# Splitting roped queries into high and low float32r parts ahead of the per-head key projection in a one-core decoder layer

## The chip, the cores and the metric

The kernel runs on one core of one Trainium2 chip. The metric is device time in microseconds (us) for one execution of the whole layer; several executions are timed and their median is compared. One more execution is taken under the hardware profiler, and all durations below come from that one.

## The reference, cut to what matters

The layer takes 1024 tokens (16 sequences of 64) of width 256 and adds three sublayers to them: self-attention over quantised weights, cross-attention with a compressed context, and a mixture of 16 experts. The change lies in the cross-attention:

```python
q_hk = (hidden_q @ Wq.T).reshape(Bv, Sv, H, K)             # 16 heads of 128
q_big = jnp.einsum('bshk,hkq->bshq', q_hk, w_kc_q)         # 192 per head
q_big = _apply_rope(q_big, sin_q, cos_q)                   # a half rotated against the other
q_r = jnp.einsum('bshq,hqr->bhsr', q_big, W_qr)            # 64 per head
k_r = jnp.einsum('bld,hdr->bhlr', kv_r, W_kr)
scores = jnp.einsum('bhsr,bhlr->bhsl', q_r, k_r)
attn = jax.nn.softmax(scores, axis=-1)
ctx_c = jnp.einsum('bhsl,bld->bhsd', attn, kv_r)
```

The kernel multiplies W_qr by W_kr ahead of time, so that the roped query of a head, 192 long, is multiplied by one 192 x 64 matrix and then meets the context itself.

## The kernel before, in words

The program runs in three stages: self-attention (to about 205 us of the span), cross-attention (to about 415 us), then routing and experts. Instructions are emitted by Python helpers in a program order; a planner that simulates the engines then fixes one order for each engine. `issue_after` and `after` pin some instructions behind others. An engine works through its own order and waits at whatever instruction is not ready. The planner may move work of the next unit ahead of work that would wait.

**Units.** Cross-attention works on a quad of four heads and a half of the tokens (512) at a time. `units` (L1117) lists eight such units. The loop at L1121 runs as a pipeline: in iteration n it computes the rotated queries of unit n (`rotated_queries`), the per-head product and scores of unit n-1 (`pair_queries`, `pair_scores`), and the context and output projection of unit n-2 (`pair_context`, `cross_project`).

**Rotated queries.** The four heads have 4 x 96 = 384 first-half and 384 second-half query entries. They are laid out in three tiles t of 128 rows, each with two halves ab. For each t and ab six float32r matmuls (a float32 product made of high and low parts, three passes for each of two chunks) fill one PSUM tile `mm`, of which there are four. VectorE multiplies it by two rope tables (`rt` tiles, L976); GpSimd subtracts or adds two of them (L982) into a float32 tile `roped`. The generator yields after each t, so the three tiles are spread over an iteration.

**Per-head product.** A head's 96 rows do not fit the 128-row tiles: tile 0 holds head 0 and the start of head 1, tile 1 the rest of head 1 and the start of head 2, tile 2 the rest of head 2 and head 3. `w_s` holds for each tile t, each of two blocks blk (the two heads in it) and each ab a 128 x 64 matrix with zeros in the rows of the other head. `pair_queries` (L988) runs 12 float32 matmuls for a unit, each of 64 output columns; the two of a (t, ab) write the two halves of the PSUM partitions. ScalarE copies the sums to `q_r` (L1008), and L1020 multiplies them by the context.

**Weights of a quad.** `quad_steps` (L403) loads six raw matrices through SyncE's queue into the single-buffered `raw` tiles, zeroes `w_s` on GpSimd (L422), makes `w_q` with L431 and the blocks of `w_s` with L453 (PE) and L463 (VectorE copies out of PSUM). Each raw tile must be released by its readers before the next quad's load.

`three` and `parts_of` (L107 to L113) are the helpers of the float32r scheme: `parts_of` copies to the high part on ScalarE and subtracts on VectorE or the engine that is named.

## Time and profile before

| | us |
|---|---|
| median of 3 runs | 569.73 (569.17 to 570.04) |
| profiled execution, its own time | 570.74 |
| its span | 569.0 |
| PE busy in the span | 537.4 |
| VectorE / ScalarE / GpSimd busy | 400.9 / 279.3 / 230.5 |
| mean granted TensorE clock | 0.984 |

The profile's page gives busy time by engine, the chain of work that ended last, and the costliest groups of instructions. A float32 matmul appears as two records, a float32r matmul as one. Two 64-column matmuls into different halves of the PSUM partitions overlap, so the mean duration of one record is longer than what a record adds. PE is TensorE, PEld its weight loads, DVE VectorE, ACT ScalarE, POOL GpSimd, SP SyncE.

### The profile page before, as it was taken

What the parts mean: (1) busy time and instruction counts of PE and PEld (TensorE: products, weight loads), DVE (VectorE), ACT (ScalarE), POOL (GpSimd) and SP (SyncE); (2) the same over time, 40 slices, a digit from 0 to 9 for tenths busy, and PEclk for the clock granted to TensorE, in tenths of its full rate; (3) what the DMA queues carried; (4) which work ended last, traced back from release to release, by engine and by line L of the source; (5) the groups of instructions that cost most, each with busy time, mean ns of one, the idle gap of its engine ahead of it and who ended that gap; (6) DMA issues with size and microseconds to landing.
All of it is one profiled execution on the core that took longest, in us unless ns stands there. A gap on an engine that the chain in (4) does not pass through costs nothing.

```text
span 569.0 us, 10603 instructions
## 1 busy us (share of the span) xinstructions
PE 537.4 (94%) x4013; PEld 444.5 (78%) x4013; DVE 400.9 (70%) x879; ACT 279.3 (49%) x524; POOL 230.5 (41%) x213
## 2 busy tenths in 40 slices
PE   7999999999999998999999999999999879999961
PEld 6888898988989876667687676676788779999961
DVE  5456555644555788767485686888878678999876
ACT  4677556575565533131323324143445368777551
POOL 4160500102000104434441445453445738888862
PEclk9999999999999999999999999999999989999995
DMA  8654431724300499564010000000322667776374
GB/s 213 163 170 129 129 106 44 205 95 108 97 1 1 119 289 277 140 188 127 2 52 20 8 1 1 0 30 1 105 106 80 209 217 255 244 249 239 123 272 164
DMA packets 44262, 70.83 MB, mean 124 GB/s; under 512 B 11824, under 2 KB 25232, under 8 KB 44208
## 3 DMA queue, kind: packets, MB, share of 16 engines
q1 hardware_dynamic: 39376, 58.71, 34.7%
q0 software_dynamic: 3696, 10.36, 4.7%
q10 hardware_dynamic: 1136, 1.05, 0.6%
q8 instruction: 33, 0.54, 0.4%
q14 instruction: 21, 0.17, 0.1%
HBM read 48.61 MB, written 21.86 MB: 124 GB/s over the span
## 4 chain that ended last, share of the span: by engine, by line
PE 76%; DVE 11%; DMA 4%; issue 3%; ACT 3%; POOL 1%; SPq 0%; DVEq 0%; ACTq 0%; POOLq 0%
PE mm L104 45%; PE mm L997 7%; PE av L582 5%; PE at L565 4%; PE av L104 3%; PE at L343 3%; PE at L1020 2%; PE av L1033 2%; PE mm L431 2%; DMA yd<-y,to 2%; ACT w L278 1%; DMA w<-in_W 1%; DVE hp L113 1%; DVE w L283 1%; DVE x L1326 1%
## 5 line engine op out<-in xcount | busy, mean ns | idle before, releaser
L982 POOL TENSOR_TENSOR roped<-rt,rt 128x512 f32<-128x512 f32 x48 | 62.6, 1326 | 83.3 <-DVE rt L976 80.4
L976 DVE TENSOR_TENSOR rt<-mm,rope_q 128x512 f32<-128x512 f32 x96 | 61.4, 684 | 24.3 <-PE mm L104 23.6
L104 PE MATMUL mm<-xn,w_q 128*128 128x512 f32 x288 | 73.9, 403 | 0.5 <-ACT xn L222 0.5
L104 PEld LDWEIGHTS mm<-xn,w_q 128*128 128x128 f32 x288 | 52.2, 188 | 14.1 <-issue 1.8
L104 PE MATMUL mm<-xs,w 128*128 128x384 f32 x270 | 54.2, 348 | 6.0 <-ACT xs L112 3.0
L1296 POOL DMA_INDIRECT yd<-y,to x45 | 48.7, 1082 | 19.4 <-ACT y L1291 8.0
L104 PEld LDWEIGHTS mm<-xs,w 128*128 128x128 f32 x270 | 47.0, 193 | 8.3 <-ACT xs L112 4.0
L327 ACT ACTIVATE p<-p 128x512 f32<-128x512 f32 x32 | 20.1, 629 | 62.3 <-DVE p L326 62.3
L324 DVE TENSOR_REDUCE sm_m<-at 128x8 f32<-128x512 f32 x32 | 21.8, 680 | 36.1 <-PE at L565 35.2
L997 PE MATMUL mm<-roped,w_s 128*64 128x512 f32 x192 | 46.4, 601 | 0.7 <-POOL roped L982 0.7
L514 POOL TENSOR_TENSOR wv<-code,scale 128x512 fp32r<-128x512 f32 x7 | 9.0, 1282 | 87.4 <-DMA scale<-in_scales 50.3
L605 DVE TENSOR_TENSOR x<-mm,x 128x256 f32<-128x256 f32 x64 | 26.0, 419 | 24.0 <-PE mm L104 22.8
L104 PE MATMUL mm<-wo,o 128*128 128x256 f32 x256 | 39.6, 295 | 0.0
L104 PE MATMUL mm<-xn,wq 128*128 128x512 f32 x128 | 34.6, 404 | 0.7 <-ACT xn L222 0.5
L104 PE MATMUL av<-w,hp 128*128 128x256 f32 x225 | 35.0, 289 | 0.3 <-ACT y L1291 0.3
L104 PE MATMUL mm<-wv,xn 128*128 128x256 f32 x256 | 35.2, 288 | 0.0
L104 PE MATMUL mm<-xn,wk 128*128 128x512 f32 x128 | 34.9, 405 | 0.0
L582 PE MATMUL av<-pt,v 128*128 128x128 f32 x256 | 34.5, 277 | 0.0
L104 PEld LDWEIGHTS mm<-wo,o 128*128 128x128 f32 x256 | 32.9, 190 | 1.5 <-issue 0.4
L582 PEld LDWEIGHTS av<-pt,v 128*128 128x128 f32 x256 | 32.0, 191 | 1.2
L104 PEld LDWEIGHTS mm<-wv,xn 128*128 128x128 f32 x256 | 31.8, 189 | 0.9
L514 POOL TENSOR_TENSOR wo<-code,scale 128x512 fp32r<-128x512 f32 x8 | 10.9, 1368 | 52.0 <-PE mm L104 39.6
(216 smaller groups left out, 1163.8 us busy)
## 6 DMA issues: line engine op xcount, KB each, us to landing
w<-in_W SPq DMA_DIRECT2D x15, 640.0 KB, 4.2
code<-in_codes SPq DMA_DIRECT2D x32, 256.0 KB, 4.4
scale<-in_scales SPq DMA_DIRECT2D x32, 256.0 KB, 4.9
xr<-xd SPq DMA_DIRECT2D x15, 408.0 KB, 4.9
xd<-zeros SPq DMA_DIRECT2D x8, 720.0 KB, 6.8
yd<-zeros SPq DMA_DIRECT2D x8, 512.0 KB, 6.6
got<-yd SPq DMA_DIRECT2D x16, 256.0 KB, 3.6
wq<-in_Wq SPq DMA_DIRECT2D x4, 512.0 KB, 3.7
```

The lines of the kernel that those rows point to most:

```text
L104: m = nc.tensor.matmul(ps, lhsT=l, rhs=r, start=(n == 0), stop=(n == len(pairs) - 1))
L324: nc.vector.tensor_reduce(m, sc, AX.X, ALU.max)
L327: exps.append(nc.scalar.activation(p, p, AF.Exp, scale=scale).ins)
L343: last = nc.tensor.transpose(ps[:, 2 * n : 2 * n + 2, :].rearrange("p a q -> p (a q)"), pn[:, 2 * n : 2 * n + 2, :].rearrange("p a k -> p ...
L514: mults[n] = eng.tensor_tensor(w, *loaded[gr].pop(n), ALU.mult).ins
L565: nc.tensor.matmul(sc[par * 64 : par * 64 + 64, 2 * g + pp, :], lhsT=qk[0][:, b * S : (b + 1) * S], rhs=qk[1][:, b * S : (b + 1) * S], sta ...
L582: nc.tensor.matmul(av[:, k * 128 : (k + 1) * 128], lhsT=v[:, i, k0 : k0 + HD], rhs=pt[:, i].rearrange("p a q -> p (a q)"), start=True, sto ...
L605: nc.vector.tensor_tensor(x[i], ps, x[i], ALU.add)
L976: nc.vector.tensor_tensor(mt, ps3, rope_table(t, 2 * ab + k), ALU.mult)
L982: nc.gpsimd.tensor_tensor(r.rearrange("p (b s) -> p b s", s=S), one, two, op)
L997: nc.tensor.matmul(ps[h // 2][(h % 2) * 64 : (h % 2) * 64 + 64], lhsT=w_s[:, t, blk, ab, :], rhs=roped[2 * t + ab], start=first[h], stop=l ...
L1296: sent = nc.gpsimd.indirect_dma_start(out=yd[: (E - 1) * SLOTS + min(TOPK, E - 1 - e) * NT], out_offset=bass.IndirectOffsetOnAxis(ap=to[:, ...
```

## The change

Tiles 0 and 2 are no longer kept in float32. After the add, GpSimd's result is split by `parts_of` into a float32r high part (`roped`, a ScalarE copy) and a low part (`ropel`, a GpSimd subtraction). For these two tiles the two 64-column blocks of a pair become one 128-column matrix, itself split into high and low parts (`w_sp`), and the product runs as three float32r passes for each ab. Tile 1, whose heads belong to different pairs, keeps its four float32 matmuls. The order of the tiles becomes 0, 2, 1. Each pair's sixth pass is issued after the matmuls of tile 1. `quad_steps` builds the 128-column matrices in the raw tile `wkq` (`whole`), and splits them from there. To make room, `c_t` has three buffers in place of four, and the on-chip scratch for dynamic transfers is set to 8192 bytes.

```diff
-            w_s = pool.tile([128, 3, 2, 2, DC], F32, tag="w_s", name="w_s")
+            w_s = pool.tile([128, 2, 2, DC], F32, tag="w_s", name="w_s")
+            t = pool.tile([128, 2, 2, 4 * DC], F32R, tag="w_sp", name="w_sp")
+            w_sp = [t[:, 0], t[:, 1]]
             nc.gpsimd.memset(w_s, 0.0)
...
+            whole = raw_tile("wkq", [128, 2, 4 * DC]).rearrange(
+                "p t (n b d) -> p t n b d", n=2, b=2
+            )
+            nc.gpsimd.memset(whole, 0.0)
...
-                        nc.vector.tensor_copy(w_s[rows, t, blk], ps[rows, t % 2, blk])
-            weights[qd] = [w_q, w_s]
+                        to = w_s[rows, blk] if t == 1 else whole[rows, t // 2, :, blk]
+                        nc.vector.tensor_copy(to, ps[rows, t % 2, blk])
+            parts_of(whole.rearrange("p t n b d -> p t (n b d)"), *w_sp)
+            weights[qd] = [w_q, (w_s, w_sp)]
...
-                for t in range(3):
+                for t in TILES:
...
-                        r = xa.tile([128, 512], F32, tag=f"roped{t}{ab}", name=f"roped{t}{ab}", bufs=1)
-                        nc.gpsimd.tensor_tensor(
-                            r.rearrange("p (b s) -> p b s", s=S), one, two, op
+                        if t == 1:
...
+                        else:
+                            nc.gpsimd.tensor_tensor(one, one, two, op)
+                            r = [
+                                xa.tile(
+                                    [128, 512], F32R, tag=f"{n}{t}{ab}", name=f"{n}{t}{ab}", bufs=1
+                                )
+                                for n in ("roped", "ropel")
+                            ]
+                            parts_of(one.rearrange("p b s -> p (b s)"), *r, nc.gpsimd)
+                        roped[t, ab] = r
...
+                ps, last = [mm_tile() for _ in range(2)], []
+                for pr in range(2):
+                    pairs = []
+                    for ab in range(2):
+                        cols = slice(ab * 2 * DC, (ab + 1) * 2 * DC)
+                        pairs += three([w[:, pr, cols] for w in w_sp], roped[2 * pr, ab])
+                    for n, (l, r) in enumerate(pairs):
+                        last.append((ps[pr], l, r))
+                        if n < 5:
+                            nc.tensor.matmul(*last.pop(), start=n == 0, stop=False)
+                for ab in range(2):
+                    for blk in range(2):
+                        nc.tensor.matmul(
+                            ps[blk][64 - 64 * blk : 128 - 64 * blk],
+                            lhsT=w_s[:, blk, ab, :],
+                            rhs=roped[1, ab],
+                            start=False,
+                            stop=False,
                         )
...
+                for t, l, r in last:
+                    nc.tensor.matmul(t, lhsT=l, rhs=r, start=False, stop=True)
...
-                    xa.tile([128, 512], F32R, tag=f"c_t{n}", name=f"c_t{n}", bufs=4)
+                    xa.tile([128, 512], F32R, tag=f"c_t{n}", name=f"c_t{n}", bufs=3)
...
-    nc = bacc.Bacc("TRN2", target_bir_lowering=False, num_devices=1)
+    nc = bacc.Bacc("TRN2", target_bir_lowering=False, num_devices=1, dynamic_dma_scratch_size=8192)
```

Other lines follow the new shapes: the raw tiles `w_last_up` and `rows1`, which borrowed `w_s`, borrow `w_sp`.

More of the change, by code (lines that the diff above doesn't have):

```diff
@@ L63 @@
 )
-BLOCK_HEADS = ((0, 1), (1, 2), (2, 3))
+TILES = (0, 2, 1)
 EARLY = {7: 1, 8: 1, 9: 1, 10: 1, 11: 1, 12: 1, 14: 1, 15: 2, 16: 2, 17: 1, 18: 2}
@@ L922, in shared_hidden @@
                 or [
-                    pool.tile([128, 512], F32R, tag=f"c_t{m}", name=f"sh{m}", bufs=4)
+                    pool.tile([128, 512], F32R, tag=f"c_t{m}", name=f"sh{m}", bufs=3)
                     for m in range(2)
@@ L980, in rotated_queries @@
                     ):
-                        r = xa.tile([128, 512], F32, tag=f"roped{t}{ab}", name=f"roped{t}{ab}", bufs=1)
-                        nc.gpsimd.tensor_tensor(
-                            r.rearrange("p (b s) -> p b s", s=S), one, two, op
-                        )
-                        roped.append(r)
-                    yield
-            def pair_queries(w_s, roped):
-                ps = [mm_tile() for _ in range(2)]
-                left = [4 if h in (1, 2) else 2 for h in range(4)]
-                first = [True] * 4
-                for t in range(3):
-                    for ab in range(2):
-                        for blk in range(2):
-                            h = BLOCK_HEADS[t][blk]
-                            left[h] -= 1
-                            nc.tensor.matmul(
-                                ps[h // 2][(h % 2) * 64 : (h % 2) * 64 + 64],
-                                lhsT=w_s[:, t, blk, ab, :],
-                                rhs=roped[2 * t + ab],
-                                start=first[h],
-                                stop=left[h] == 0,
-                            )
-                            first[h] = False
+                        if t == 1:
+                            r = xa.tile(
+                                [128, 512], F32, tag=f"roped{t}{ab}", name=f"roped{t}{ab}", bufs=1
+                            )
+                            nc.gpsimd.tensor_tensor(
+                                r.rearrange("p (b s) -> p b s", s=S), one, two, op
+                            )
+                        else:
[3 more added lines that the diff above has]
+                                    [128, 512], F32R, tag=f"{n}{t}{ab}", name=f"{n}{t}{ab}", bufs=1
+                                )
+                                for n in ("roped", "ropel")
+                            ]
+                            parts_of(one.rearrange("p b s -> p (b s)"), *r, nc.gpsimd)
@@ new lines, in rotated_queries, with pair_queries @@
+                        roped[t, ab] = r
+                    yield
+            def pair_queries(w_s, w_sp, roped):
+                ps, last = [mm_tile() for _ in range(2)], []
[16 more added lines that the diff above has]
+                            stop=False,
+                        )
+                for t, l, r in last:
+                    nc.tensor.matmul(t, lhsT=l, rhs=r, start=False, stop=True)
@@ L1067, in dense_weights @@
                 ]
-                up = xb.tile([128, 3, 2, 2, DC], F32, tag="w_s", name="w_last_up")
+                up = xb.tile([128, 2, 2, 4 * DC], F32, tag="w_sp", name="w_last_up")
                 down = xb.tile([128, 2, D], F32, tag="w_o0", name="w_last_down")
                 for t, cols in (
-                    (up.rearrange("p a b c d -> p (a b c d)"), slice(0, W_UP)),
+                    (up.rearrange("p a b c -> p (a b c)")[:, :W_UP], slice(0, W_UP)),
                     (down.rearrange("p a b -> p (a b)"), slice(W_UP, W_COLS)),
@@ L1125, in decoder_layer @@
                     next(prep)
-                roped[n] = []
+                roped[n] = {}
                 qd, half = units[min(n, len(units) - 1)]
@@ L1130, in decoder_layer @@
                 if n - 1 in here:
-                    q_rs = pair_queries(weights[units[n - 1][0]][1], roped.pop(n - 1))
+                    q_rs = pair_queries(*weights[units[n - 1][0]][1], roped.pop(n - 1))
                 c_ts = [pair_context(pt, units[n - 2][1]) for pt in pts_n]
@@ L1185, in decoder_layer @@
                     rows[1] = [
-                        xw.tile([128, 3, 2, 2, DC], F32, tag="w_s", name="rows1")
-                        .rearrange("p a b c d -> p (a b c d)")[:, : 2 * ROW]
+                        xw.tile([128, 2, 2, 4 * DC], F32, tag="w_sp", name="rows1")
+                        .rearrange("p a b c -> p (a b c)")[:, : 2 * ROW]
                         .rearrange("p (a b) -> p a b", a=2)
```

## The prediction

> **What bounds the kernel now.** I read the page first: which engine is full, what the ending chain is made of, and what the edited lines cost.

> ```profile
> PE 537.4 (94%) x4013; PEld 444.5 (78%) x4013; DVE 400.9 (70%) x879; ACT 279.3 (49%) x524; POOL 230.5 (41%) x213
> ...
> PE 76%; DVE 11%; DMA 4%; issue 3%; ACT 3%; POOL 1%; SPq 0%; DVEq 0%; ACTq 0%; POOLq 0%
> ...
> L982 POOL TENSOR_TENSOR roped<-rt,rt 128x512 f32<-128x512 f32 x48 | 62.6, 1326 | 83.3 <-DVE rt L976 80.4
> ...
> L997 PE MATMUL mm<-roped,w_s 128*64 128x512 f32 x192 | 46.4, 601 | 0.7 <-POOL roped L982 0.7
> ```

> PE carries 76% of the chain. The product to be changed (L997) is 46.4 us of PE and hardly waits; its supplier on POOL has 83.3 us of slack. An average hides stages, so next the table of windows, here one late iteration of the cross-attention loop, its start and its end:

> ```profile
> 224.00:250.00 26.00, 25.31 (x173) 16.76 (x171) 21.31 (x41) 6.31 (x12) 15.64 (x13) 1.00 0.56 163
> ...
> 342.80:364.60 21.80, 21.80 (x159) 15.38 (x158) 16.64 (x31) 7.21 (x12) 11.01 (x8) 1.00 0.00 1
> ...
> 390.20:415.00 24.80, 23.68 (x187) 16.61 (x187) 21.04 (x78) 10.93 (x19) 10.96 (x10) 1.00 0.29 95
> ```

> Columns are the stretch, then busy PE, PEld, DVE, ACT, POOL. PE is busy for the whole iteration, so PE time taken out there is taken from the span unless a wait replaces it. The chain of waits, in order of time, gives PE's prices:

> ```profile
> 229.61 3.00 PE mm L104 x12
> ...
> 325.64 2.80 PE mm L104 x12
> ...
> 342.81 3.64 PE mm L997 x16
> ...
> 350.97 1.87 PE mm L997 x8
> ```

> A float32r pass of 128 x 512 is 2.80/12 = 0.233 us; directly after 64-column work (229.61) the same 12 take 3.00, so that switch costs 0.2. Eight records of L997 (four float32 matmuls) take 1.87, sixteen 3.64: 5.51 per unit.

> **The change part by part.** The sum is made against the profiled execution (span 569.0, own time 570.74); the median, 569.73, lies 1.0 below that, and I apply the difference to it.

> *PE.* Per unit, tiles 0 and 2 lose sixteen records (3.64) and gain 12 passes (2.80); tile 1 keeps 1.87. The two postponed passes follow tile 1's 64-column work: +0.2 at most. Gain 0.64 to 0.84 per unit, I take 0.70: **-5.6** for eight units (-5.1 to -6.7). [...]

> *GpSimd.* Four subtractions per unit, 32 in all, at the 1.28 of L982: +41 us on POOL, which has 21.8 - 11.0 = 10.8 us free in the late iteration against 5.1 added. Six adds, four subtractions and two softmax products (1.04 each) make 14.9 per unit. Three instances from POOL's timeline place them:

> ```profile
> 343.05 1.04 POOL L334 TENSOR_TENSOR pn<-p,sm_s 128x512 f32<-128x512 f32 x1 [2.24 <-DVE sm_s L330]
> 344.06 3.91 POOL L982 TENSOR_TENSOR roped<-rt,rt 128x512 f32<-128x512 f32 x2
> ...
> 351.15 2.51 POOL L982 TENSOR_TENSOR roped<-rt,rt 128x512 f32<-128x512 f32 x2 [3.19 <-DVE rt L976]
> ...
> 359.10 2.55 POOL L982 TENSOR_TENSOR roped<-rt,rt 128x512 f32<-128x512 f32 x2 [5.44 <-DVE rt L976]
> ```

> The first tile starts at 351.15 and, with two more subtractions, ends at 356.3. The second (now tile 2) starts at 359.10 and ends at 364.2. The next product starts on PE at 364.63, and takes five passes of tile 0 (1.2 us) before it needs tile 2: slack 1.6. The third tile, now tile 1, needs only its adds. They come some 4.5 us after the product's start, covered by ten passes (2.3), the transposes (1.0) and next queries (2.8). So in the middle units I charge 0.3 in all (0 to 3.0). If the cover is gone, each wait lands on PE whole. Behind a subtraction stand the softmax products in POOL's queue; PE's transposes of the next iteration need those 4 us or more later.

> [...] Above, the pair at 344.06 took 3.91 in place of 2.5 beside such an instruction (a split of a raw weight). But L976 reads PSUM and stays at 684 ns on average, though POOL often works beside it. If every product were to suffer like that pair, 32 subtractions would each lose 0.7, some 22 us of POOL time; by the rows only the four new weight splits do. I go with the rows.

> *Start (units 0 and 1).* Here POOL is on the chain already:

> ```profile
> 223.79 3.77 POOL roped L982 x3
> 227.60 2.00 PE mm L997 x8
> ```

> POOL's first four adds run from 222.54 to 227.56. With four subtractions the same two tiles end at 232.6. PE can bring forward 12 query passes (2.8 to 3.0), quad 2's L431 work (3.0) and five passes of tile 0 (1.2) from 225.0, which reaches 232; but the product now holds two of the four `mm` tiles to its end, where the first was free after sixteen records. **+1.5** (0.5 to 4.0).

> *End (unit 7).* No further queries follow as cover, and the chain goes through DVE:

> ```profile
> 391.21 0.68 DVE rt L976
> 391.89 0.85 DVE limit L732
> ...
> 397.14 0.60 DVE sm_m L324
> ```

> Before, the first pair's sums were complete after sixteen records and its softmax began at 397.14. Now both pairs complete with the last two passes, about 7 us after the last query matmul at 390.2; copy (0.59) and scores (1.1) put that start near 399.2. DVE has about 1 us of routing work to put in the hole. **+1.3** (0 to 2.5).

> *ScalarE.* 32 high copies at some 0.6 (the row of `c_t` copies is 587 ns), 2.4 per unit where it is 33% busy: nothing of its own; as a link in POOL's chain it is in the range. *Quads.* Four splits (ScalarE 0.6, DVE 0.69), the memset of `whole` on POOL behind L431, L463's copies behind that memset. GpSimd clears 256 + 512 elements in place of 768 (0.74 us): the same. Quads 2 and 3 have an iteration as cover; quad 1's split lies near 208 us, where DVE leads to the stage's start: **+0.3** (0 to 1.4). On SP's queue the next `wkq` load waits for the split, 2 to 3 us later, ahead of `wqr`, `wkr`, table loads and zeroing writes; quad 2's weights are not used until 233, so nothing. *Three `c_t` buffers.* Each iteration takes two, and the last projection is done some 14 us before the next context; nothing. *Smaller scratch.* No row shows its fill. 77 indirect transfers are issued about 1.26 us apart at the closest and land in 4.3 us: about four in flight. [...] It can hardly help and I take nothing; a stall of each to its landing would be 45 x 3 = 135 us, which I leave out for that count.

> Sum: -5.6 + 1.5 + 1.3 + 0.3 + 0.3 = **-2.2**: span 566.8, median **567.5**. The ends are -5.1 + 4.0 + 2.5 + 3.0 + 1.4 = +5.8 and -6.7 + 0.5 = -6.2: 563.5 to 575.5.

> **The rivals.** *A, slower: the handoff POOL to ScalarE to POOL ends last.* If POOL keeps program order, each half is add (1.28), a wait for the copy (some 0.9 with its two handoffs), subtraction: the second tile takes 6.9 instead of 5.1, and 8.0 with a softmax product between. It then ends 2.4 after the product's start, and PE waits up to 1.2. At 0.9 for seven units this is 6.3 in place of 0.3: +3.8, **573.5**. It decides from about 0.35 per unit, where the sum is zero. For it: POOL and ScalarE work in fixed order, and in the list of waits ScalarE's queue already stands up to 6.6 us behind a `q_r` copy. Against it: the planner can interleave the halves, and PE has next queries to pull forward.

> *B, no change: start and end cost what the middle gains.* With the start at 4 and the end at 1.3 the sum is +0.3: **570.0**. For it: PE had already pulled work forward there; against it: 3 us of L431 are ready.

> *C, all of the gain:* the planner fills start and end: -6.2, **563.5**.

> *D, not what it says:* if float32r passes with weights from `w_sp` ran slower than query passes, for instance 0.30, twelve are 3.6 and the gain is gone; with start and end +3.4, 573.1. The same operation in the same shape makes this unlikely; it is within A's share.

> **How the numbers follow.** What I describe 0.40 (its own range 565.2 to 568.5), C 0.12: both faster by over 0.2%, 0.52. B 0.14. A with D 0.34. Within 0.2% means 1.1 us here, about what a measurement of this kernel can tell from no change. The range takes in both ends, 563.5 to 575.5.

> **What would show it.** Right: product records worth 4.7 to 4.9 us per unit in the chain; twelve new 128 x 512 passes at 0.23; POOL near 272 us busy in all with L976 unchanged; late iterations of about 21.1 us, PE full. The start should be 1 to 2 us longer. Wrong: PE waiting on `ropel` in the middle units by more than 0.35 per unit (A), an idle PE of 3 to 4 us between 224 and 236 (B), or transfers in the expert stage that issue late.

## The result and the profile after

The changed kernel takes **575.81 us** (575.18 to 576.07) where the kernel before takes 569.59 (569.17 to 570.04) beside it: a ratio of 1.0105 (95% interval 1.0093 to 1.0117), so it is 1% slower. The prediction was 567.5 with a range of 563.5 to 575.5; direction and range were both wrong. The profiled execution of after took 575.18, 0.6 below its median, with a span of 573.3.

The page of after first: busy time, the shares of the ending chain, and the groups that the change made. L999 are the adds of tiles 0 and 2 (L982 before), L114 the new subtractions, L986 the products with the rope tables (L976 before).

```profile
PE 537.0 (94%) x3981; PEld 452.7 (79%) x3981; DVE 407.2 (71%) x883; ACT 297.6 (52%) x560; POOL 269.5 (47%) x249
...
PE 82%; DVE 8%; ACT 3%; DMA 2%; issue 2%; POOL 1%; SPq 0%; DVEq 0%; ACTq 0%; POOLq 0%
...
L986 DVE TENSOR_TENSOR rt<-mm,rope_q 128x512 f32<-128x512 f32 x96 | 61.6, 684 | 25.5 <-PE mm L105 24.5
...
L999 POOL TENSOR_TENSOR rt<-rt,rt 128x512 f32<-128x512 f32 x32 | 40.5, 1287 | 45.3 <-DVE rt L986 45.2
...
L114 POOL TENSOR_TENSOR ropel<-rt,roped 128x512 fp32r<-128x512 f32 x32 | 40.7, 1288 | 5.9 <-ACT roped L113 5.7
```

PE should have lost 5.6 us of work and lost 0.4 (part of what it does now runs at a clock of 0.50 in place of 1.00, as will be seen). The 32 subtractions cost what was predicted (1.288 us each), and L986 did not slow down (684 ns, as before). So the new work was priced rightly; what PE does around it was not. The windows say where: the start (from the first query matmul to unit 1's product) after and before, then, after alone, one late iteration and the stretch from unit 7's product to the first dense matmul. Columns as in the prediction, then the granted clock.

```profile
216.84:255.25 38.41, 34.78 (x189) 24.80 (x189) 28.10 (x56) 11.43 (x22) 26.39 (x23) 0.91 0.57 163
...
215.32:250.09 34.77, 34.08 (x212) 23.85 (x212) 28.85 (x61) 9.01 (x17) 18.12 (x15) 1.00 0.66 198
...
349.51:371.02 21.51, 21.51 (x153) 16.38 (x153) 17.80 (x31) 9.09 (x16) 13.78 (x11) 1.00 0.00 1
...
397.00:432.50 35.50, 32.57 (x258) 26.65 (x256) 29.62 (x100) 14.17 (x24) 13.99 (x13) 1.00 0.22 79
```

The last two took 21.82 and 34.90 before. The late iteration gained 0.31 where 0.70 was expected. The start lost 3.6; PE stood idle for 3.63 us of it (38.41 - 34.78; before 0.69), and the clock column reads 0.91 where it was 1.00. Starts of PE's work, read from its timeline, in us:

| | first query matmul | product of unit 1 | of unit 2 | of unit 7 | first dense matmul |
|---|---|---|---|---|---|
| before | 215.3 | 250.1 | 270.5 | 390.2 | 425.1 |
| after | 216.8 | 255.2 | 277.2 | 397.0 | 432.5 |
| difference, running | +1.5 | +5.1 | +6.7 | +6.8 | +7.4 |

Nearly all of the loss is there before unit 2, and units 2 to 6, where the gain was to be made, make none. Now the place of the idle time, in four windows of 3 us, and what stood there in the timeline:

```profile
226.00:229.00 3.00, 1.54 (x8) 0.81 (x7) 3.00 (x4) 0.58 (x1) 3.00 (x3) 1.00 1.02 267
229.00:232.00 3.00, 0.91 (x3) 0.73 (x3) 3.00 (x6) 2.11 (x4) 3.00 (x3) 0.50 1.00 263
232.00:235.00 3.00, 3.00 (x8) 2.32 (x8) 0.64 (x2) 0.00 (x0) 3.00 (x4) 0.50 1.02 276
235.00:238.00 3.00, 3.00 (x12) 2.39 (x12) 1.39 (x3) 0.00 (x0) 0.89 (x1) 0.87 0.51 131
```

```profile
226.20 2.39 DVE L193 TENSOR_SCALAR ln_x<-x,ln_rstd,ln_shift 128x256 f32<-128x256 f32 x2
...
227.12 2.60 POOL L999 TENSOR_TENSOR rt<-rt,rt 128x512 f32<-128x512 f32 x2
...
229.69 3.73 POOL L114 TENSOR_TENSOR ropel<-rt,roped 128x512 fp32r<-128x512 f32 x3
...
231.17 0.79 PE L1022 MATMUL mm<-roped,w_sp 128*128 128x512 f32 x1 [2.09 <-ACT roped L113]
...
231.76 2.76 PE L105 MATMUL mm<-xn,w_q 128*128 128x512 f32 x6
...
235.93 1.57 PE L105 MATMUL mm<-xn,w_q 128*128 128x512 f32 x6
```

POOL works without a gap; PE waits 2.09 us for the first pass of tile 2; and when it has work again it runs slower: six query passes take 2.76, where the next six, from 235.93 on, take 1.57. The clock of 0.50 lasts from 229 to about 235.8 (the last row's mean of 0.87 is 0.8 us at 0.50).

The late iteration in the chain of waits shows why its gain is small:

```profile
349.51 2.31 PE mm L1022 x10
351.82 0.88 PE at L344 x8
352.70 2.81 PE mm L105 x12
355.51 1.87 PE mm L1025 x8
357.38 0.66 PE mm L1033 x2
358.04 1.90 PE av L1062 x32
359.94 0.42 PE mm L105
360.36 1.02 PE at L1049 x16
361.39 2.77 PE mm L105 x11
364.15 1.02 PE at L1049 x16
365.18 5.85 PE mm L105 x36
```

The product is 2.31 + 1.87 + 0.66 = 4.84, against 5.51: the predicted 0.67. But its last two passes (L1033, 128 columns) now stand between tile 1's product and the context (both 64 columns). The context takes 1.90 instead of 1.75, the scores 1.02 + 1.02 instead of 0.87 + 1.02, the 24 query passes 6.00 instead of 5.80; the transposes win 0.15 back. -0.67 + 0.15 + 0.15 + 0.20 - 0.15 = -0.32, which is the measured 0.31.

### The profile page after: what moved, and what is told of

Read it like the earlier page. It is cut to its first block, busy times and chain, and to the rows that moved or that the text cites. A ratio compares the mean times of both kernels' runs of the same rounds, so it can differ in the third digit from the quotient of the medians.

```text
span 573.3 us, 10632 instructions
## 1 busy us (share of the span) xinstructions
PE 537.0 (94%) x3981; PEld 452.7 (79%) x3981; DVE 407.2 (71%) x883; ACT 297.6 (52%) x560; POOL 269.5 (47%) x249
## 4 chain that ended last, share of the span: by engine, by line
PE 82%; DVE 8%; ACT 3%; DMA 2%; issue 2%; POOL 1%; SPq 0%; DVEq 0%; ACTq 0%; POOLq 0%
PE mm L105 49%; PE av L592 5%; PE av L105 5%; PE at L575 4%; PE mm L1022 3%; PE mm L1025 3%; PE at L344 2%; PE av L1062 2%; PE mm L435 2%; PE at L1049 2%; ACT w L279 1%; PE at L1286 1%; DMA scale<-in_scales 1%; PE mm L461 1%; DVE rt L986 1%
## 5 line engine op out<-in xcount | busy, mean ns | idle before, releaser
L986 DVE TENSOR_TENSOR rt<-mm,rope_q 128x512 f32<-128x512 f32 x96 | 61.6, 684 | 25.5 <-PE mm L105 24.5
L105 PE MATMUL mm<-xn,w_q 128*128 128x512 f32 x288 | 76.1, 408 | 0.7 <-ACT xn L223 0.5
L999 POOL TENSOR_TENSOR rt<-rt,rt 128x512 f32<-128x512 f32 x32 | 40.5, 1287 | 45.3 <-DVE rt L986 45.2
L325 DVE TENSOR_REDUCE sm_m<-at 128x8 f32<-128x512 f32 x32 | 21.9, 683 | 35.6 <-PE at L575 34.9
L114 POOL TENSOR_TENSOR ropel<-rt,roped 128x512 fp32r<-128x512 f32 x32 | 40.7, 1288 | 5.9 <-ACT roped L113 5.7
L524 POOL TENSOR_TENSOR wo<-code,scale 128x512 fp32r<-128x512 f32 x8 | 10.9, 1365 | 51.6 <-PE mm L105 38.9
L105 PE MATMUL mm<-xn,wk 128*128 128x512 f32 x128 | 34.9, 405 | 0.0
L592 PE MATMUL av<-pt,v 128*128 128x128 f32 x256 | 34.5, 277 | 0.0
```

Source lines behind the costliest of these rows:

```text
L105: m = nc.tensor.matmul(ps, lhsT=l, rhs=r, start=(n == 0), stop=(n == len(pairs) - 1))
L114: return (eng or nc.vector).tensor_tensor(lo, src, hi, ALU.subtract).ins
L325: nc.vector.tensor_reduce(m, sc, AX.X, ALU.max)
L524: mults[n] = eng.tensor_tensor(w, *loaded[gr].pop(n), ALU.mult).ins
L592: nc.tensor.matmul(av[:, k * 128 : (k + 1) * 128], lhsT=v[:, i, k0 : k0 + HD], rhs=pt[:, i].rearrange("p a q -> p (a q)"), start=True, sto ...
L986: nc.vector.tensor_tensor(mt, ps3, rope_table(t, 2 * ab + k), ALU.mult)
```

## The experiments

My theory after the result: the POOL chain of unit 0 is the loss; with it a slow clock, and a displaced weight split. The rivals: the float32r product itself, the ScalarE copies, the smaller scratch, or the late normalisation of half 1 that leads the chain. r1, p1, p2 and d1 ran on a chip with a longer and less steady expert stage for every kernel, the one before included (578.21); for these the start of the first dense matmul (425.1 before, 432.5 after) says more than the ratio (r1, the kernel before but for buffers and scratch, reached it at 426.3 there). z1, l1, m1, w1, q1, c1 and c2 were executed once each, so their times carry no interval. Stretches inside the profiles repeat much better than whole runs: from the first query matmul to unit 7's product the kernel before, r1, s1, s2 and s3 all take 174.9 us.

**Is it scratch or buffers?** The kernel before, with both:

```diff
-... name=f"c_t{n}", bufs=4)
+... name=f"c_t{n}", bufs=3)
-    nc = bacc.Bacc("TRN2", ..., num_devices=1)
+    nc = bacc.Bacc("TRN2", ..., num_devices=1, dynamic_dma_scratch_size=8192)
```

> The kernel before with three c_t buffers and the 8192-byte scratch, nothing else. Theory (the loss is made where units 0 and 1 start and where quad 1's weights are split): within 0.6 us of the kernel before. Rival (fewer buffers or the small scratch hold back projections or indirect transfers): slower by 2 us or more, with GpSimd's transfers issuing later in the expert stage.

Measured: 576.62 against 578.21, 0.9973 (0.9933 to 1.0013). The interval was too wide for the question whether a small gain hides there, and the profiles raised it: from the first expert matmul to PE's end took 111.9 us before and 108.5 after. So each part was run alone, again in the kernel before: scratch 8192, scratch 4096, and three `c_t` buffers.

> The kernel before with the scratch for dynamic transfers set to 8192 and nothing else. If the smaller scratch is what shortens the expert stage: 567 to 568.5 us in place of about 569.8, a ratio of 0.996 to 0.998, and 109 to 110 us from the first expert matmul to PE's end in place of 111.9. Rival (the expert stage gains by the other order of instructions, or the single profile of before was long by chance): ratio 0.999 to 1.001. [...]

> The kernel before with the scratch at 4096. A gain from a smaller scratch would be as large or larger than with 8192 (ratio 0.995 to 0.998); the rival gives 0.999 to 1.001; a stall of the indirect transfers, which the prediction had bounded and left out, should show here first, with transfers in the expert stage that issue late and a ratio above 1.005.

> The kernel before with three c_t buffers and the full scratch. Each iteration takes two and the last projection is done before the next context, so nothing: ratio 0.999 to 1.001. If the third buffer is where r1's 0.997 came from, 0.996 to 0.998.

Measured: 0.9990 (0.9979 to 1.0002), 0.9993 (0.9984 to 1.0001) and 0.9995 (0.9986 to 1.0004). None is a cause, and even 4096, half of what the change sets, stalls nothing. The expert stretch takes 111.2, 111.0 and 111.4 in these three, so its shorter time after the change (107.8 to 109.6 in seven of the eight kernels of the new form on such chips, 111.0 in the eighth) does not come from the scratch or the buffers. The changed kernel has another order of instructions there too; which part of that order saves the 2 to 3 us was not isolated.

**Which of the new operations?** Three variants of the changed kernel. p1 lets GpSimd write the sum as float32r once and uses that tile for both parts (no copy, no subtraction); p2 keeps the ScalarE copy and leaves the subtraction out; d1 moves all 32 subtractions to VectorE. In p1 and p2 the low part of the queries is missing and the high part stands in its place.

```diff
-                            parts_of(one.rearrange("p b s -> p (b s)"), *r, nc.gpsimd)
+                            nc.scalar.copy(r, one.rearrange("p b s -> p (b s)"))     # p2
+                            r = [r, r]                                               # p2
+                            parts_of(one.rearrange("p b s -> p (b s)"), *r)          # d1
```

> The changed kernel without the split of the queries: GpSimd writes the sum as float32r and this one tile stands for both parts, so the low part is left out; TensorE runs the same passes with the same weights. Theory: TensorE's form gains about 0.3 us per unit net of its switches between 64 and 128 columns (-2.6), quad 1's weight split costs 1.5: 568.6, and the stretch from the first query matmul to unit 1's product is as long as in the kernel before (34.9 us). Rival (the passes or the weights are what is slow): 573 or more.

> The changed kernel with the ScalarE copy to the high part but no GpSimd subtraction; the high part stands for the low one too. Theory (the queue of subtractions and ScalarE's order both delay the first units): about 570, between the changed kernel and the one without any split. Rival (GpSimd's time alone is the cost): the same as without any split, 568.6. Rival (ScalarE's copies, held behind other copies in its fixed order, are the cost): 574 or more.

> The changed kernel with all 32 subtractions on VectorE (0.7 us each, 22 us) in place of GpSimd. Theory (GpSimd's queue[...] delay the first units): 571 to 573, since VectorE takes half the time for each but leads the chain at the start and the end. Rival (the handoff through ScalarE is the cost, whoever subtracts): 575 or more.

| | time against 578.21 | ratio | start of the stage | first dense matmul |
|---|---|---|---|---|
| p1, no copy, no subtraction | 574.69 | 0.9953 (0.9907 to 0.9999) | 33.4 | 424.2 |
| p2, no subtraction | 578.89 | 1.0027 (0.9965 to 1.0088) | 33.2 | 425.6 |
| d1, subtraction on VectorE | 586.47 | 1.0154 (1.0101 to 1.0207) | 38.9 | 434.8 |

The start of the stage is the stretch from the first query matmul to unit 1's product, 34.8 before and 38.4 after. By the dense matmul the copies cost 1.4 us and the subtractions 6.9 (432.5 - 425.6). With p1's start displaced by the same 1.5 as after's, the product's form is worth 0.9 + 1.5 = 2.4 net: the form gains. d1 missed, and its time is where its rival, the handoff through ScalarE, had put it: VectorE is no better place. In d1's start VectorE is busy for 34 of the 38.9 us. But the copies alone do not make the start's loss, since p2 keeps them and its start is 33.2.

**Is it unit 0 alone?** The changed kernel without the subtraction in unit 0, whose low part is left out; the other 28 subtractions stay.

```diff
+                            if low:
                                 parts_of(one.rearrange("p b s -> p (b s)"), *r, nc.gpsimd)
+                            else:
+                                nc.scalar.copy(r[0], one.rearrange("p b s -> p (b s)"))
+                                r = [r[0], r[0]]
```

> The changed kernel, but unit 0 (the first of eight) gets no subtractions: its high part stands for its low part, so its low part is left out; the other seven are as changed. Theory (the start alone costs the five us): from the first query matmul to unit 1's product 33.5 to 34.5 us (changed kernel 38.4, before 34.8), and the granted clock of that stretch back at 1.00. Rival (every unit's subtractions hold TensorE, spread out): 37 or more there.

Measured: 566.49 against 570.18 beside it. Its start:

```profile
216.90:250.10 33.20, 32.29 (x189) 23.41 (x189) 28.69 (x58) 12.03 (x23) 21.24 (x18) 1.00 0.67 189
```

33.2 us in place of after's 38.4, PE idle for 0.9, the clock at 1.00. Four subtractions of 1.29 us decide the sign of the change up to the first dense matmul: 424.5 here, 425.1 before, 432.5 after. The rest of z1's lead over the kernel before, about 3 us, lies in the shorter expert stage.

**Which link of that stretch?** The chain of after is led by VectorE: `ln_x` of half 1 at 226.20, 2.40 us, then the copies `xn` and `roped` on ScalarE. If that were the cause, moving it would help. l1 takes half 1's normalisation off VectorE; m1 emits it an iteration later; w1 moves the weight split's subtraction from VectorE to GpSimd, which undoes the displacement by 1.5; q1 goes the other way and adds only POOL work to the kernel before: four subtractions in unit 0 that nobody reads.

```diff
-                if k % 2:                                                            # l1
+                if k % 2 and not (which == 2 and half == 1):
-                if n == 0:                                                           # m1
+                if n == 1:
-            parts_of(whole.rearrange("p t n b d -> p t (n b d)"), *w_sp)             # w1
+            parts_of(whole.rearrange("p t n b d -> p t (n b d)"), *w_sp, nc.gpsimd)
+                        if busy and t < 2:                                           # q1
+                            nc.gpsimd.tensor_tensor(one, one, two, ALU.subtract)
```

> The changed kernel with the four row normalisations of the second token half, which fall into unit 0, all on ScalarE; before, two were on VectorE, and in the changed kernel those two took 2.40 us beside GpSimd's subtractions in place of 0.74. Theory (VectorE waits for GpSimd there, ScalarE's high copies wait behind the copies that follow it): the stretch shortens by 1.5 to 3 us, to 35.5 to 37. Rival (GpSimd's queue of subtractions is long enough by itself): 38 or more.

> The changed kernel with the whole normalisation of the second token half moved from unit 0's iteration to unit 1's. Theory (it is the meeting of this work with the subtractions that opens the hole on TensorE): the stretch from the first query matmul to unit 1's product is 35 to 37 us, and part of the gain is given back in the next iteration. Rival (GpSimd's queue by itself): 38 or more.

> The changed kernel with the subtraction of the four weight splits on GpSimd in place of VectorE. Theory (quad 1's split lies in VectorE's chain ahead of the first query matmul): that matmul starts 0.6 to 1.5 us earlier than 216.8, between 215.3 and 216.2, and the rest is as in the changed kernel. Rival (the shift comes from the copies waiting for the cleared tile, not from the subtraction): it stays at 216.5 or later.

> The kernel before with four extra GpSimd subtractions in unit 0 (two after the adds of tile 0, two after those of tile 1), whose results nobody reads. It adds GpSimd's occupancy alone, without a handoff through ScalarE and without a reader on TensorE. Theory (the hole is opened by occupancy[...] and what queues behind it): from the first query matmul to unit 1's product 36.5 to 38.5 us, where before has 34.8, and the normalisation on VectorE again takes over 1 us each. Rival (the chain of copy and subtraction that TensorE waits for is needed): 34.8 to 35.8.

| | time | before beside it | start of the stage | clock in it |
|---|---|---|---|---|
| l1 | 576.13 | 570.18 | 35.5 | 1.00 |
| m1 | 576.48 | 570.18 | 38.9 | 0.91 |
| w1 | 574.20 | 570.18 | 38.3 | 0.91 |
| q1 | 573.51 | 569.85 | 38.8 | 0.96 |

m1 tells nothing: the planner left `ln_x` where it was (226.78). l1's start is as short as was expected if `ln_x` were the cause; but its clock stayed up, and against c2 below, where it also stayed up, it is only 0.9 shorter. Its time did not follow, in part because its clock fell later, so that the stretch from unit 7's product to the first dense matmul took 37.0 in place of 35.4:

```profile
399.43:402.84 3.41, 3.41 (x9) 1.16 (x6) 2.48 (x23) 0.22 (x1) 0.00 (x0) 0.50 0.02 5
```

w1 and q1 tell most. In w1 the first query matmul is back at 215.3, and `ln_x` at its old place and price:

```profile
219.85 0.74 DVE L193 TENSOR_SCALAR ln_x<-x,ln_rstd,ln_shift 128x256 f32<-128x256 f32 x2
```

and still the stretch takes 38.3; the kernel z1, on the other hand, has the late and slow form (226.27, 2.40 us) and loses nothing. So the `ln_x` that leads after's chain is not what the loss hangs on. With it out of the way POOL is what leads; w1's timeline:

```profile
224.98 1.28 POOL L114 TENSOR_TENSOR ropel<-rt,roped 128x512 fp32r<-128x512 f32 x1
...
226.21 2.50 POOL L999 TENSOR_TENSOR rt<-rt,rt 128x512 f32<-128x512 f32 x2
...
228.66 3.75 POOL L114 TENSOR_TENSOR ropel<-rt,roped 128x512 fp32r<-128x512 f32 x3
...
229.41 0.80 PE L1022 MATMUL mm<-roped,w_sp 128*128 128x512 f32 x1 [3.19 <-ACT roped L113]
...
230.00 2.76 PE L105 MATMUL mm<-xn,w_q 128*128 128x512 f32 x6
```

PE has query passes whose `xn` was written by 226.6, but they stand in its order behind the first pass of tile 2, and that waits for a copy, which waits for an add that POOL does after a subtraction. VectorE's next rope products wait 2.2 us for the subtraction too, since it still reads the `rt` tile that they overwrite:

```profile
229.96 1.29 DVE L986 TENSOR_TENSOR rt<-mm,rope_q 128x512 f32<-128x512 f32 x2 [2.20 <-POOL ropel L114]
```

q1 shows that no handoff to ScalarE is needed for this. In the kernel before, with only POOL fuller:

```profile
228.85 1.89 DVE L976 TENSOR_TENSOR rt<-mm,rope_q 128x512 f32<-128x512 f32 x3 [1.63 <-POOL rt L987]
...
230.09 3.60 PE L999 MATMUL mm<-roped,w_s 128*64 128x512 f32 x8 [2.98 <-POOL roped L982]
```

**The clock.** l1 and w1 both have one gap of 3.19 us on PE (in w1 a pass of 0.50 and 0.76 of idle time stand ahead of it), but l1's clock stayed at 1.00 there and its start was 2.8 shorter. To change the clock alone, eight spare float32r passes, never read, were put behind half 1's transposes; c1 and c2 differ only in the PSUM tile that the passes write.

```diff
+                    spare = av_tile()              # c1; c2: at_tile([128, 512])
+                    with tc.issue_after(turned[-1]):
+                        for _ in range(8):
+                            nc.tensor.matmul(spare, lhsT=..., rhs=xn_t[0][0][:, 0, :], start=True, stop=True)
```

> The changed kernel with eight spare float32r passes of 128 x 512 (1.9 us of TensorE, result read by nobody) put behind the transposes of the second token half, where TensorE otherwise stands idle in unit 0's product. It adds work to the fullest engine. Theory (the idle stretch lets the granted clock fall to a half, and that is some 3 us of the loss): the clock stays at 1.00 and the stretch from the first query matmul to unit 1's product falls from 38.6 to 35.5 to 36.5 us. Rival (the clock figure is a by-product and only the idle time costs): 38.4 or longer.

> The changed kernel with eight spare float32r passes (128 x 512, result unread) right behind the transposes of half 1, as in the previous one but into a tile of the transposes' PSUM pool, which should be free at once; so they should lie at about 229 to 231 us, where the changed kernel's PE stands idle. Theory (part of the loss at the start is a TensorE clock that fell to 0.50 because PE stood idle): the clock between 229 and 236 us stays at or near 1.00, the stretch from the first query matmul to the first product of unit 1 falls from 38.4 to 35.5 to 37 us, and the run is 2 to 3 us below 574.5. Rival (the clock is no cause; the chain of the other engines sets the time and the PE's clock only stretches work that had slack): the clock stays up but the stretch remains at 38 us or more.

c1 (574.52 against 570.37) was inconclusive: its tile was still being read by VectorE, so the passes began at 230.62, when the clock had already fallen. c2 put them at 228.81. First c1's windows of 3 us, then c2's with its whole start:

```profile
229.00:232.00 3.00, 1.65 (x5) 1.19 (x5) 3.00 (x6) 2.11 (x4) 3.00 (x3) 0.75 0.98 262
232.00:235.00 3.00, 3.00 (x10) 2.37 (x9) 0.45 (x1) 0.00 (x0) 3.00 (x4) 0.68 1.02 273
```

```profile
229.00:232.00 3.00, 2.78 (x13) 1.92 (x12) 2.95 (x6) 2.10 (x4) 3.00 (x3) 1.00 1.02 275
232.00:235.00 3.00, 3.00 (x14) 2.41 (x13) 1.58 (x3) 0.00 (x0) 3.00 (x4) 1.00 1.01 272
...
216.81:253.10 36.29, 34.53 (x195) 24.58 (x196) 28.07 (x56) 11.28 (x22) 26.44 (x23) 1.00 0.60 173
```

VectorE, ScalarE and POOL run as in after to within 0.05 us up to 231, and tile 2's first pass starts at the same time (231.15; after 231.17). With the clock at 1.00 the start is 36.3 in place of 38.4, unit 7's product starts at 394.9 in place of 397.0, the first dense matmul at 430.3 in place of 432.5, and the run takes 573.44 (569.41 beside it). So 2.1 us of the loss is the clock. The trace of after agrees, with PE busy for 4.73 us at the low clock; an estimate of what that costs is half of it, 2.4, by the clock of 0.50, or 2.0 by the six query passes (4.73 x (2.76 - 1.57) / 2.76):

```profile
228.98:235.80 6.82, 4.73 (x12) 3.66 (x12) 4.46 (x8) 2.11 (x4) 6.82 (x6) 0.50 1.00 272
```

The price is shown by this; that the spare passes are what kept the clock up is likely, but not shown by one run, since l1 kept it through a gap of 3.19 us without them. The rest of the start, 36.3 against z1's 33.2, is PE waiting behind POOL: without the spare passes PE stands idle for 3.9 us of c2's start (36.29 - 34.53 + 2.12), in z1's for 0.9.

**A version without the loss.** b1 keeps unit 0 in float32: its products use the unsplit 128-column matrix, kept in a tile of its own, so unit 0 needs no subtraction. The weight splits subtract on GpSimd as in w1, and the scratch is 6144 to make room.

```diff
-                        if t == 1:
+                        if t == 1 or plain:                          # plain: unit 0
...
+                        if plain:
+                            pairs.append((whole_0[0][:, pr, cols], roped[2 * pr, ab]))
+                        else:
-                        pairs += three([w[:, pr, cols] for w in w_sp], roped[2 * pr, ab])
+                            pairs += three([w[:, pr, cols] for w in w_sp], roped[2 * pr, ab])
```

> A version meant to keep the gain and drop the loss: unit 0 keeps float32 queries for tiles 0 and 2 and multiplies them by the unsplit 128-column matrix (kept in a tile of its own, scratch 6144 bytes to make room), the other seven units are split as changed, and the weight splits subtract on GpSimd. Theory: first query matmul at 215.3, unit 1's product 34 to 35 us later, every later unit some 0.3 us shorter than before: 0.3% to 0.8% faster than the kernel before. Rival (the subtractions hold every unit): same as before or slower.

Measured: 566.59 against 569.85, **0.9948 (0.9931 to 0.9964)**: faster than both kernels. The first query matmul came at 216.0, where 215.3 was expected. PE's line of the page, and the window of its start:

```profile
PE 531.9 (94%) x3977; PEld 450.5 (80%) x3977; DVE 403.4 (71%) x879; ACT 295.2 (52%) x556; POOL 270.2 (48%) x249
```

```profile
216.00:250.00 34.00, 32.56 (x185) 22.68 (x185) 27.25 (x58) 9.59 (x19) 21.11 (x18) 1.00 0.67 190
```

PE's 531.9 is 5.5 below before's 537.4; an estimate from the profile of before puts 1.6 of this to its expert stage, where PE was busy for 3.2 us at a clock of 0.50 (465.2 to 468.6), which b1's was not. The start no longer loses. But the 0.5% is not the product's: b1 reaches the first dense matmul at 424.1, 0.9 before the kernel before, and the other 3.5 us between the two profiles lie in the expert stage, whose gain was not traced to its cause.

## Why the prediction was wrong, step by step

**The start, +1.5: the step that failed.** From the first query matmul to unit 2's product the changed kernel takes 60.3 us (277.17 - 216.84), the kernel before 55.2. With the product's gain for two units (2 x 0.67) added back, the start costs 6.5, beyond the bound of 4.0. Leaving the subtractions out of unit 0 alone (z1) brings the 60.3 to 55.5, so 4.8 hang on these four; leaving out all of them (p2) brings it to 54.7. The last 0.8 or so was not isolated. Its first half was right: POOL was to end the two tiles at 232.6, and ended at 233.4. What failed is the cover: 12 query passes, quad 2's L431 work and five passes of tile 0, which "reaches 232". Work that is ready is not work that runs: PE follows its order, and there the query passes stood behind tile 2's first pass, and L431's work (L435 now) at 239. Between 226.04 and 231.17 PE ran one product pass and six transposes. The prediction had named that sign itself, an idle PE of 3 to 4 us, under rival B.

**The clock: a term that was not in the sum.** The profile of before had 1.00 in every window shown, and the idle time of a rival was priced only by its length. By c2, 58.3 us to unit 2's product, 2.1 of the 4.8 is the clock, and the other 2.7 the wait. What makes the clock fall was not shown. It stayed at 0.50 for 6.8 us in after and for 3.4 in c1 (1.5 and 1.9 in its two rows) and in l1 (399.43 to 402.84); the means over the start, 0.96 in q1 and 0.91 in w1 and m1, give about 3 and 7 us there, as an estimate. In after it fell at 229, and PE had not been idle throughout before that: from 226.04 to 229 its waits were broken by a pass and the transposes (1.54 us busy in 226 to 229). Of two gaps of equal length (3.19 us) w1's lost the clock and l1's did not; w1's fell at about 227.4, 1.2 us into the gap. l1's fell at 399.4, after a gap of 2.02 us that after has too (2.01, at 399.5) and passed at 1.00. So the length of a gap alone does not tell. The sum of the prediction had nothing for the clock; the measurement says 2.1.

**PE, -5.6.** Size of the product right (4.84 per unit, within the 4.7 to 4.9 named; passes of 1.16 / 5 = 0.23). The step was incomplete: it charged the switch to 64 columns and back inside the product only, and two postponed passes made new switches for the neighbours. Over units 2 to 6 PE changes between 64-column and wider work 38 times before, 46 after and 42 in z1, counted matmul by matmul. At 0.15 to 0.20 a change, an estimate for the 8 more is 1.2 to 1.6 of 5 x 0.67 = 3.35, and for 4 it is 0.6 to 0.8; PE's busy time in these units is 119.6, 118.2 and 117.0. That is read off the profiles; a product without postponed passes was not tried.

**Units 2 to 6, +0.3.** Rival A's place: the view of the `ropel` tiles names no idle time of PE before the 32 passes that read one, so the handoff did not decide there. Still the five take 119.8 us against 119.7 before, where 3 less were due: of 3.35 PE gave back 1.9 in other work, most of it switches, and stood idle for 1.5, 1.3 of it in the last iteration, where the chain stands on ScalarE between 380.5 and 385 (copies `q_r`, `roped`, `xn`). "Nothing of its own" was too low for ScalarE: p2 against p1 puts the copies at 1.4 in all. z1 has the same code for these units and needs 117.6, so this part of the loss hangs on the order that the planner made, not on the work.

**Quad 1's weights, +0.3: it was +1.5,** just over its bound of 1.4. The new subtraction was put on VectorE, the engine that leads there; on GpSimd (w1) the first query matmul is back at 215.3.

**The end, +1.3: right.** From unit 7's product to the dense stage 35.4 against 34.8, with a product gain of 0.7 in it. The way was right too: the softmax of the first pair begins 9.7 us after that product's start (406.74 - 397.02), before 6.8; the prediction had it at 9.0. The size hangs on the planner's order as well: z1, with the same passes, takes 34.5. **Scratch and buffers, nothing: right** (s1, s2, s3). **POOL's rows: right** (269.5 busy where 272 was named).

**The sum.** To the first dense matmul: +1.5 for the weights, +5.1 for units 0 and 1 (their own product gain included), +0.2 for units 2 to 6, +0.6 for the end: +7.4. The prediction had -2.2 there, and nothing behind it; from the first dense matmul to PE's end the changed kernel takes 3.4 us less (131.8 against 135.2), which no term named and no run explains. That hid part of the loss by luck: the medians differ by 6.2. Rival B named the place, but neither the size nor the clock, and not that the middle would gain nothing.

## What to carry to other kernels

Work moved to an idle engine is free only where something else on the bottleneck's own order can run while that engine finishes; look at the first pass through a pipeline, where there is no earlier unit to cover it, and give it another form if need be (b1 did so, and reached the first dense matmul 8.3 us earlier than the changed kernel). When a gap opens on TensorE, look at the granted clock behind it: work done while the clock is down adds to the gap's own length (2.1 us here, with the clock at 0.50), and a run with spare matmuls in the gap can tell the two apart (c2). And the work that leads the chain need not be the cause: in w1 it was out of the way, and the time stayed.
